# Spreading per-head values over partitions by DMA through DRAM instead of by matmul

## The chip, the core and the metric

The kernel runs on one core of one Trainium2 chip. The metric is the device time of one execution in microseconds (us), the median of three runs. A profile comes from one further execution, whose own time and span are given beside it. The core has five engines with a queue each: PE (TensorE, matmuls; its weight loads are listed as PEld), DVE (VectorE), ACT (ScalarE), POOL (GpSimd) and SP (SyncE), which here only issues DMAs.

## The reference, cut to what matters

The input `x` is 64 graphs of 256 tokens by 512 features, in float32, and `adj` is one 256x256 mask for each graph. Two graph-attention layers follow one another, each added to its input:

```python
h = relu(layernorm(x));  m = h @ map_w.T                 # layer 0, 8 heads of 64
n = m_head / max(norm(m_head), 1e-8)
cos_adj = ((n @ n.T) * keep > 0.1)
p = softmax(where(adj, -1e10, q @ k.T / 8)) * keep
x = x + relu(((cos_adj * p) @ sem) @ gcn_W.T / ((cos_adj * p).sum(-1) + 1))
h = relu(layernorm(x))                                   # layer 1, 4 heads of 64
x = x + (softmax(where(adj, q1 @ k1.T / 8, -max)) @ v1) @ Wo + bo
```

Two quantities belong to a head and a token and have to reach all 64 features of that head: the inverse length of a head in layer 0, by which `m` is multiplied to give `n`, and the inverse sum of the softmax in layer 1.

## The kernel before, in words

Everything is held with features (or keys) on the 128 partitions and the 256 tokens along the free axis, so the two heads of a chunk lie on partitions 0 to 63 and 64 to 127. Layer 0 has four chunks of two heads, layer 1 has two.

The graphs go through a software pipeline, written out by hand in `period(i)` (L535 to L662). One period works on four graphs: layer 1's attention of graph i-1 (`b`), layer 0's attention of graph i (`g`), the projections of graph i+1 (`nx`), and loading and normalising graph i+2 (`n2`). The scheduler is off (`tc.manual_schedule()`, L668): each engine runs its instructions in the order in which the program writes them, and waits at its head for whatever that instruction needs. In the trace a period in the middle of the run lasts from 1819.11 to 1877.92 us.

PSUM is one ring of eight banks (`ring`, L172; `bank`, L178). Tiles take the banks in turn, so a new tile waits until the tile eight allocations earlier has been read for the last time.

The order of PE in a period, with the lines that matter here:

- `sc1`: layer 1's scores of `b` (`products`, L384). ACT takes their exponentials (L391), and DVE masks them (L398).
- `p_b`: `spread(g)` (L357). Four matmuls against a selection matrix `sel` carry the inverse lengths `rn` of graph i to all partitions, into two banks; DVE multiplies `mT` by them into `nT` (L367).
- `p_m`, then `sc`: the first product of `mapped(nx)`, then layer 0's scores of `g`. ACT takes exponentials, DVE masks them (L400), POOL adds the two halves of each (`d`, L404).
- the rest of `mapped(nx)`. `seven_products` computes a 2x2 block product with seven matmul groups. Three of them add up in one bank, named `_z`; DVE reads that bank out between them (L291, L309), and the next group may only start when it has.
- `co`: the cosines `nT` x `nT` (L421). They take eight banks. DVE compares and multiplies (L434).
- queries of `nx`, the squares and `p_n` (their sums per head, `norms`, L350: four matmuls with 32 output columns each).
- `av` of layer 1 (`values1`) and `zb` (`sums1`, L514): layer 1's sums of `b`. `zb` is four matmuls against ones of 64 columns, so that each sum stands on all 64 partitions of its head. ACT copies it to `b.z` (L522), and `divided(b)` (L524) takes a reciprocal of 128x512 on DVE (L526) and multiplies `avs1` (L527).
- `av` and `sm` of layer 0, then the first product of `keys(nx)`, `sums_back` and `heads_back` (`p_l`, L483). For `heads_back` DVE makes `o` (L485), and POOL adds it to `xs` (L487, two instructions).
- the other products of `keys(nx)` (`p_k_z`, `p_k`), with `result(b)` (`p_o`, L532) among them. Its input is `avs1`.
- layer 1's projections of `g`, and the transposes of `n2`.

SP's queue in a period holds, in this order: four transposing DMAs `far` (L437), two transposing DMAs `mask` for `n2` (L327, which wait for `adb` of POOL, L322), the output of `b` (L636), and the loads of graph i+3 (L188, L190). The load into `xs` waits until the output has landed, since it reuses that buffer.

Of the kernel before, what the change touches and what calls it, by code (L numbers as in the profile page):

```python
# [8 lines left out]
F32 = mybir.dt.float32  # L9
# [19 lines left out]
class Weights:  # L29
# [4 lines left out]
    def __init__(self, nc, const, a):  # L34
        P, D, DH = 128, a["x"].shape[2], 64
        self.nc, self.const, self.a = nc, const, a
        self.ident = const.tile([P, P], F32, name="ident")
        make_identity(nc, self.ident)

        self.gt = const.tile([P, P], F32, name="gt")  # L40
        nc.vector.memset(self.gt, 0.0)
        for j in range(2):
            nc.scalar.dma_start(out=self.gt[j * DH:(j + 1) * DH, j * DH:(j + 1) * DH], in_=a["gcn_WT"])
        self.gb = const.tile([P, D // P], F32, name="gb")
        nc.scalar.dma_start(out=self.gb, in_=a["gcn_map_b"].rearrange("(c p) -> p c", p=P))
# [10 lines left out]
        self.sel = const.tile([P, 2, P], F32, name="sel")  # L56
        for j in range(2):
            nc.vector.memset(self.blk32[j * DH:(j + 1) * DH, j * 16:(j + 1) * 16], 1.0)
            for k in range(2):
                r = 32 * k + 16 * j  # L60
                nc.vector.tensor_add(self.sel[:, k, j * DH:(j + 1) * DH], self.ident[:, r:r + 1].to_broadcast([P, DH]),
                                     self.ident[:, r + DH:r + DH + 1].to_broadcast([P, DH]))
# [90 lines left out]
def fast_path(ctx, tc, a, w, chk, out):  # L153
# [4 lines left out]
    nc = tc.nc  # L158
# [2 lines left out]
    P, DH = 128, 64  # L161
    H0, NKC = D // DH, D // P
    INNER = a["Wq"].shape[1]
    NIC = INNER // P
    NT = S // P
    SCALE = DH ** -0.5

# [1 line left out]
    sb2 = ctx.enter_context(tc.tile_pool(name="sb2", bufs=2))  # L169
    sb1 = ctx.enter_context(tc.tile_pool(name="sb1", bufs=1))  # L170
    small = ctx.enter_context(tc.tile_pool(name="small", bufs=4))
    ring = ctx.enter_context(tc.tile_pool(name="ring", bufs=8, space=bass.MemoryType.PSUM))  # L172

    x_t = x.rearrange("b (t p) d -> b p t d", p=P)
# [3 lines left out]
    def bank(name, shape=(P, 2, S), dtype=F32):  # L178
        return ring.tile(list(shape), dtype, tag="bank", name=name)
# [173 lines left out]
    def lengths(g, p):  # L353
        g.rn = sb1.tile([P, S], F32, tag="rn", name=f"rn{g.i}")
        nc.vector.tensor_scalar_max(g.rn, p, COS_EPS * COS_EPS)

    def spread(g):  # L357

        ps = [bank(f"p_b{g.i}_{h}") for h in range(2)]
        for k in range(2):  # L360
            for h in range(2):
                r = slice(h * DH, (h + 1) * DH)
                nc.tensor.matmul(ps[h][:, k, :], w.sel[r, k, :], g.rn[r, :], start=True, stop=True)
        g.nT = sb1.tile([P, NKC, S], F32, tag="nT", name=f"nT{g.i}")
        for h in range(2):
            c = slice(2 * h, 2 * h + 2)
            nc.vector.tensor_mul(g.nT[:, c, :], g.mT[:, c, :], ps[h])  # L367

    def queries(g):
        g.qT = sb1.tile([P, NKC, S], F32, tag="qT", name=f"qT{g.i}")  # L370
# [108 lines left out]
    def heads_back(g):  # L479
        for t in range(NT):  # L480
            p = bank(f"p_l{g.i}_{t}", [P, NKC, P])
            for c in range(NKC):
                nc.tensor.transpose(p[:, c, :], g.avs[:, c, t * P:(t + 1) * P], w.ident)  # L483
            o = sb2.tile([P, H0, DH], F32, tag="xn", name=f"o{g.i}_{t}")
            nc.vector.tensor_mul(o, p.rearrange("p c (h d) -> p (c h) d", d=DH),  # L485
                                 g.rk[:, t, :, None].to_broadcast([P, H0, DH]))
            nc.gpsimd.tensor_add(g.xs[:, t, :], g.xs[:, t, :], o.rearrange("p h d -> p (h d)"))  # L487
# [8 lines left out]
    def values_in(g, t):  # L496
        if t == 0:
            g.v = sb1.tile([P, NT, INNER], F32, tag="v", name=f"v{g.i}")
            g.p_v = bank(f"p_v{g.i}", [P, NT, INNER])
        for c in range(NKC):  # L500
            nc.tensor.matmul(g.p_v[:, t, :], g.h1T[:, c, t * P:(t + 1) * P], w.wv1[:, c, :],  # L501
                             start=(c == 0), stop=(c == NKC - 1))
        if t == NT - 1:
            nc.vector.tensor_copy(g.v, g.p_v)
# [7 lines left out]
        nc.scalar.copy(b.avs1, av)  # L512

    def sums1(b):  # L514
        zb = bank(f"zb{b.i}")
        for c in range(NIC):
            last = NT - 1 if b.last else 0
            for m in range(last + 1):
                for s in range(2):
                    part = b.e1[c][:, s, m * S:(m + 1) * S] if b.last else b.d1[c][:, s, :]  # L520
                    nc.tensor.matmul(zb[s * DH:(s + 1) * DH, c, :], w.ones, part, start=(m == 0), stop=(m == last))
# [13 lines left out]
    def period(i):  # L535
# [8 lines left out]
        if b:  # L544
# [123 lines left out]
    with tc.manual_schedule():  # L668
# [36 lines left out]
            next(step)  # L705
        nc.scalar.activation(g.rn, g.rn, AF.Sqrt)
        nc.vector.reciprocal(g.rn, g.rn)
        if B > 1:
            edges(graphs[1])
            normal(1)  # L710
        nc.scalar.activation(spare[:, 1:], spare[:, :1], AF.Exp)
        for _ in range(4):
            next(s)
        if B > 1:
            normal_input(graphs[1])
        for i in range(B + 1):
# [299 lines left out]
```

## Time and profile before

| | |
|---|---|
| time, median of 3 runs | 3835.53 us (3833.66 to 3836.0) |
| the profiled execution: its own time, and its span | 3832.88 us, 3831.2 us |
| PE busy | 3786.6 us (99% of the span) |
| DVE, ACT, POOL busy | 2961.6, 1614.9, 2331.2 us |
| granted TensorE clock, mean | 0.997 |
| `p_b` (L363): PE busy, and DVE's multiplication (L367) | 66.0 us, 81.4 us in 128 |
| `zb` (L521) in 63 periods | 65.8 us |
| reciprocal 128x512 (L526) in 63 periods | 210.8 us, 3346 ns each |

The page gives for each group of instructions the busy time, the mean of one, and how long the engine stood idle before them. A busy PE only says that matmuls were in flight. The chain that ended last is followed back from the end, at each step to what released it; its shares say which engine set the pace. "Issue to landing" of a DMA is the time from its instruction on SP to the last increment of its semaphore. In the timeline the columns are start, length, engine, line, operation, output<-input, shape and count; in brackets stands the idle time before it and what ended it. Instructions that follow one another on an engine overlap there by some 0.08 us.

### The profile page before, as it was taken

How to read it: one execution, taken by the hardware profiler on the slowest of the kernel's cores; microseconds unless marked ns; L12 is line 12 of the kernel's file. 1: busy time of each engine (PE TensorE's matmuls, PEld its weight loads, DVE VectorE, ACT ScalarE, POOL GpSimd, SP SyncE). 2: the span in 40 equal slices, each digit the busy share in tenths (PEclk: the TensorE clock that was granted, in tenths of full speed). 3: DMA queues.
4: the chain of work that ended last, by engine and by line, in shares of the span. 5: the costliest groups of instructions: out<-in, count | busy, mean ns of one | idle time of the engine just before them, and what ended most of it. 6: DMA issues, size and time to landing. Idle time of an engine off the chain costs nothing.

```text
span 3831.2 us, 76121 instructions
## 1 busy us (share of the span) xinstructions
PE 3786.6 (99%) x30161; PEld 3215.8 (84%) x30161; DVE 2961.6 (77%) x5420; ACT 1614.9 (42%) x4108; POOL 2331.2 (61%) x2044
## 2 busy tenths in 40 slices
PE   8999999999999999999999999999999999999997
PEld 7888888888888888888888888888888888888885
DVE  6777777787777777877877778778777787787775
ACT  2444444444344444444444444444444444444443
POOL 3656566566565665665666656656666566566562
PEclk9999999999999999999999999999999999999999
DMA  3010000001101000011011000110010101101100
GB/s 96 24 31 20 30 27 26 30 21 31 31 21 29 27 26 30 21 31 30 21 28 31 22 30 21 31 30 21 29 33 20 30 21 31 30 21 30 32 14 21
DMA packets 171305, 108.05 MB, mean 28 GB/s; under 512 B 132673, under 2 KB 137281, under 8 KB 170945
## 3 DMA queue, kind: packets, MB, share of 16 engines
q1 hardware_dynamic: 168672, 103.09, 9.3%
q8 instruction: 241, 3.95, 0.4%
q14 instruction: 120, 0.97, 0.1%
q10 hardware_dynamic: 2272, 0.04, 0.0%
HBM read 44.34 MB, written 33.55 MB: 20 GB/s over the span
## 4 chain that ended last, share of the span: by engine, by line
PE 97%; DVE 1%; DMA 1%; issue 0%; POOL 0%; ACT 0%; SPq 0%; DVEq 0%; ACTq 0%
PE sc L384 9%; PE av L411 9%; PE p_q L266 6%; PE p_k L266 6%; PE p_m L266 6%; PE p_qk L266 6%; PE p_v L501 6%; PE p_o L532 6%; PE p_s L261 6%; PE p_m_z L266 5%; PE co L421 5%; PE p_s_z L261 5%; PE p_qk_z L266 4%; PE p_k_z L266 4%; PE p_q_z L266 4%; PE p_t L220 3%
## 5 line engine op out<-in xcount | busy, mean ns | idle before, releaser
L404 POOL TENSOR_TENSOR d<-e 128x512 f32<-128x512 f32 x382 | 659.5, 1753 | 85.3 <-DVE e L400 77.3
L244 POOL TENSOR_TENSOR sh<-hT 128x256 f32<-128x256 f32 x128 | 93.1, 728 | 766.3 <-ACT hT L221 766.3
L400 DVE TENSOR_TENSOR e<-e,mask 128x1024 f32<-128x1024 f32 x256 | 443.2, 1751 | 40.2 <-ACT e L391 40.2
L446 POOL TENSOR_TENSOR d<-d,e 128x512 f32<-128x512 f32 x252 | 320.9, 1273 | 222.0 <-DVE e L444 222.0
L391 ACT ACTIVATE e<-sc 128x512 f32<-128x512 f32 x768 | 389.8, 619 | 31.2 <-PE sc L384 31.2
L487 POOL TENSOR_TENSOR xs<-xs,o 128x512 f32<-128x512 f32 x128 | 159.8, 1271 | 362.3 <-DVE o L485 362.3
L439 POOL TENSOR_TENSOR d<-d,e 128x512 f32<-128x512 f32 x252 | 311.7, 1268 | 0.0
L398 DVE SCALAR_TENSOR_TENSOR e<-mask,e 128x1024 f32<-128x1024 bf16 x128 | 189.3, 1517 | 150.1 <-ACT e L391 150.1
L221 ACT ACTIVATE hT<-p_t 128x512 f32<-128x512 f32 x256 | 139.0, 595 | 390.1 <-PE p_t L220 390.1
L434 DVE SCALAR_TENSOR_TENSOR e<-co,e 128x256 f32<-128x256 f32 (+1 forms) x1024 | 276.6, 346 | 0.3 <-ACT up L431 0.3
L431 ACT ACTIVATE up<-co,below 128x128 bf16<-128x128 f32 x512 | 159.7, 363 | 241.1 <-PE co L421 235.3
L501 PE MATMUL p_v<-wv,hT 128*128 128x256 f32 x1024 | 242.2, 379 | 0.0
L384 PE MATMUL sc<-qT,kT 64*128 64x256 f32 x2048 | 239.0, 383 | 0.0
L532 PE MATMUL p_o<-wo,own 128*128 128x512 f32 x512 | 232.1, 596 | 3.1 <-DVE own L527 3.1
L411 PE MATMUL av<-e,sem 128*64 128x256 f32 x2048 | 232.1, 379 | 0.0
L444 DVE SCALAR_TENSOR_TENSOR e<-far,e 128x256 f32<-128x256 bf16 x256 | 229.5, 897 | 0.0
L512 ACT COPY own<-av 128x512 f32<-128x512 f32 x64 | 37.4, 585 | 455.3 <-PE av L411 442.0
L211 DVE TENSOR_SCALAR xn<-xs,mv,rs 128x512 f32<-128x512 f32 x256 | 229.0, 935 | 0.1
L526 DVE RECIPROCAL own<-own 128x512 f32<-128x512 f32 (+1 forms) x65 | 214.3, 3297 | 5.8 <-ACT own L522 5.8
L384 PEld LDWEIGHTS sc<-qT,kT 64*128 64x128 f32 x2048 | 193.1, 187 | 28.1 <-DVE nT L367 0.6
L198 DVE BATCH_NORM_STATS2 st<-xs 128x6 f32<-128x512 f32 x256 | 174.4, 681 | 52.5 <-POOL xs L487 49.4
L411 PEld LDWEIGHTS av<-e,sem 128*64 128x64 f32 x2048 | 147.2, 137 | 74.3 <-issue 0.6
(197 smaller groups left out, 9336.8 us busy)
## 6 DMA issues: line engine op xcount, KB each, us to landing
xs<-in_x_dram SPq DMA_DIRECT2D x64, 512.0 KB, 3.7
out_dram<-xs SPq DMA_DIRECT2D x63, 512.0 KB, 2.7
ad<-in_adj_dram SPq DMA_DIRECT2D x64, 64.0 KB, 3.5
far<-up SPq DMA_TRANSPOSE x256, 2.3
mask<-adb SPq DMA_TRANSPOSE x128, 2.3
wm<-in_L_gnn_map_w_dram SPq DMA_DIRECT2D x4, 256.0 KB, 3.3
gw<-in_L_gnn_gcn_map_w_dram SPq DMA_DIRECT2D x2, 512.0 KB, 5.5
wq<-in_L_gnn_q_w_dram SPq DMA_DIRECT2D x4, 256.0 KB, 6.4
```

What stands on the lines that cost most here:

```text
L261: nc.tensor.matmul(region, src[:, c, :], wt[:, block, c, :], start=p not in opened, stop=True, skip_group_check=True)
L266: nc.tensor.matmul(region[:, f, :], wt[:, block, c, f * P:(f + 1) * P], src[:, c, :], start=p not in opened, stop=True, skip_group_check=True)
L384: nc.tensor.matmul(ps[s][:, j, :], rows[h, c, j * P:(j + 1) * P], cols[h, c, :], start=True, stop=True)
L391: nc.scalar.activation(e[:, s, :], p.rearrange("p j q -> p (j q)"), AF.Exp, scale=SCALE)
L400: nc.vector.tensor_mul(e, e, m)
L404: nc.gpsimd.tensor_add(d, e[:, :, :S], e[:, :, S:])
L411: nc.tensor.matmul(av[s * DH:(s + 1) * DH, n, :], vs[:, j, (h0 + s) * DH:(h0 + s + 1) * DH], q[:, s, j * S:(j + 1) * S], start=(j == 0), s ...
L434: nc.vector.scalar_tensor_tensor(e, p.rearrange("p j q -> p (j q)")[:, lo:hi], THRESHOLD, e, op0=ALU.is_gt, op1=ALU.mult)
L439: nc.gpsimd.tensor_add(g.d[c], g.d[c], g.e[c][:, :, :S])
L446: nc.gpsimd.tensor_add(g.d[c], g.d[c], g.e[c][:, :, S:])
L501: nc.tensor.matmul(g.p_v[:, t, :], g.h1T[:, c, t * P:(t + 1) * P], w.wv1[:, c, :], start=(c == 0), stop=(c == NKC - 1))
L532: nc.tensor.matmul(p, b.avs1[:, c, t * P:(t + 1) * P], w.wo1[:, c, :], start=(c == 0), stop=(c == NIC - 1))
```

## The change

Both matmul spreads go. A new helper `by_head` writes one row for each head to DRAM and reads it back with the row repeated over 64 partitions, in two DMAs, one for each half of the partitions. All three DMAs stand on SP, and the two reads need the write to have landed.

- `spread` is now three DMAs: 8 rows of `rn` to DRAM, and two reads of 256 KB into `nT`. It is called at the end of period i-1, after the reciprocal of `nx.rn`, and so stands on SP after the loads of graph i+2. The multiplication is a new `units`: one DVE instruction of 128x1024, in place on `nT`, after the last `values_in` of the period.
- `sums1` has the form of `norms`: four matmuls of 32 columns into a bank of 128x256. ACT copies that to `rz`, DVE takes a reciprocal of 128x256, and `by_head` brings 4 rows to `b.z` with two reads of 128 KB. These DMAs stand on SP after the two `mask` transposes.
- `divided` is only the multiplication, and stands after `heads_back(g)`, ahead of the second product of `keys(nx)`.
- The check value of `b` is taken from `rz`. The constants `sel` go. Two fewer PSUM banks are taken in a period.

```diff
+    def by_head(rows, step, dst, name):
+        n = P // step
+        by = dram.tile([n // 2, 2, S], F32, tag=f"by{step}", name=f"by_{name}")
+        nc.sync.dma_start(out=by.rearrange("c s q -> (c s) q"), in_=rows[::step, :])
+        for s in range(2):
+            nc.sync.dma_start(out=dst[s * DH:(s + 1) * DH], in_=by[None, :, s, :].to_broadcast([DH, n // 2, S]))
+
     def spread(g):
-        ps = [bank(f"p_b{g.i}_{h}") for h in range(2)]
-        for k in range(2):
-            for h in range(2):
-                r = slice(h * DH, (h + 1) * DH)
-                nc.tensor.matmul(ps[h][:, k, :], w.sel[r, k, :], g.rn[r, :], start=True, stop=True)
         g.nT = sb1.tile([P, NKC, S], F32, tag="nT", name=f"nT{g.i}")
-        for h in range(2):
-            c = slice(2 * h, 2 * h + 2)
-            nc.vector.tensor_mul(g.nT[:, c, :], g.mT[:, c, :], ps[h])
+        by_head(g.rn, 16, g.nT, f"rn{g.i}")
+
+    def units(g):
+        nc.vector.tensor_mul(g.nT, g.nT, g.mT)
...
     def sums1(b):
-        zb = bank(f"zb{b.i}")
-        for c in range(NIC):
-            last = NT - 1 if b.last else 0
-            for m in range(last + 1):
-                for s in range(2):
-                    part = b.e1[c][:, s, m * S:(m + 1) * S] if b.last else b.d1[c][:, s, :]
-                    nc.tensor.matmul(zb[s * DH:(s + 1) * DH, c, :], w.ones, part, start=(m == 0), stop=(m == last))
-        nc.scalar.activation(b.z, zb, AF.Copy, accum_out=chk[:, b.i, 2:3])
+        zb = bank(f"zb{b.i}", [P, S])
+        last = NT - 1 if b.last else 0
+        for m in range(last + 1):
+            for h in range(H1):
+                c, s = divmod(h, 2)
+                part = b.e1[c][:, s, m * S:(m + 1) * S] if b.last else b.d1[c][:, s, :]
+                nc.tensor.matmul(zb[32 * h:32 * (h + 1), :], w.ones[:, :32], part, start=(m == 0), stop=(m == last))
+        b.rz = sb1.tile([P, S], F32, tag="rz", name=f"rz{b.i}")
+        nc.scalar.activation(b.rz, zb, AF.Copy, accum_out=chk[:, b.i, 2:3])
+        nc.vector.reciprocal(b.rz, b.rz)
+        by_head(b.rz, 32, b.z, f"rz{b.i}")

     def divided(b):
-        for q in (slice(0, P), slice(P, S)) if b.last else (slice(0, S),):
-            nc.vector.reciprocal(b.z[:, :, q], b.z[:, :, q])
-            nc.vector.tensor_mul(b.avs1[:, :, q], b.avs1[:, :, q], b.z[:, :, q])
+        nc.vector.tensor_mul(b.avs1, b.avs1, b.z)
...
-        if g:
-            spread(g)
         if nx:
             m, s = mapped(nx), messages(nx)
...
             sums1(b)
-            divided(b)
...
         if b:
-            nc.scalar.activation(b.z, b.z, AF.Copy, accum_out=chk[:, b.i, 3:4])
+            nc.scalar.activation(b.rz, b.rz, AF.Copy, accum_out=chk[:, b.i, 3:4])
         if g:
             sums_back(g)
             heads_back(g)
+        if b:
+            divided(b)
         if nx:
             next(k)
...
             nc.vector.reciprocal(nx.rn, nx.rn)
+            spread(nx)
...
+        if nx:
+            units(nx)
         if n2:
             normal_input(n2)
```

More of the change, by code (lines that the diff above doesn't have):

```diff
@@ L55, in __init__ @@
         nc.vector.memset(self.blk32, 0.0)
-        self.sel = const.tile([P, 2, P], F32, name="sel")
         for j in range(2):
             nc.vector.memset(self.blk32[j * DH:(j + 1) * DH, j * 16:(j + 1) * 16], 1.0)
-            for k in range(2):
-                r = 32 * k + 16 * j
-                nc.vector.tensor_add(self.sel[:, k, j * DH:(j + 1) * DH], self.ident[:, r:r + 1].to_broadcast([P, DH]),
-                                     self.ident[:, r + DH:r + DH + 1].to_broadcast([P, DH]))
         self.two = const.tile([P, 2, 32], F32, name="two")
@@ L163, in fast_path @@
     INNER = a["Wq"].shape[1]
-    NIC = INNER // P
+    H1, NIC = INNER // DH, INNER // P
     NT = S // P
@@ L171, in fast_path @@
     small = ctx.enter_context(tc.tile_pool(name="small", bufs=4))
+    dram = ctx.enter_context(tc.tile_pool(name="dram", bufs=2, space=bass.MemoryType.DRAM))
     ring = ctx.enter_context(tc.tile_pool(name="ring", bufs=8, space=bass.MemoryType.PSUM))
@@ L355, in lengths @@
         nc.vector.tensor_scalar_max(g.rn, p, COS_EPS * COS_EPS)
-    def spread(g):
-        ps = [bank(f"p_b{g.i}_{h}") for h in range(2)]
-        for k in range(2):
-            for h in range(2):
-                r = slice(h * DH, (h + 1) * DH)
-                nc.tensor.matmul(ps[h][:, k, :], w.sel[r, k, :], g.rn[r, :], start=True, stop=True)
+    def by_head(rows, step, dst, name):
[4 more added lines that the diff above has]
+            nc.sync.dma_start(out=dst[s * DH:(s + 1) * DH], in_=by[None, :, s, :].to_broadcast([DH, n // 2, S]))
+    def spread(g):
         g.nT = sb1.tile([P, NKC, S], F32, tag="nT", name=f"nT{g.i}")
-        for h in range(2):
-            c = slice(2 * h, 2 * h + 2)
-            nc.vector.tensor_mul(g.nT[:, c, :], g.mT[:, c, :], ps[h])
+        by_head(g.rn, 16, g.nT, f"rn{g.i}")
+    def units(g):
+        nc.vector.tensor_mul(g.nT, g.nT, g.mT)
     def queries(g):
@@ L707, in fast_path @@
         nc.vector.reciprocal(g.rn, g.rn)
+        spread(g)
         if B > 1:
@@ L713, in fast_path @@
             next(s)
+        units(g)
         if B > 1:
```

## The prediction

> **What bounds the kernel now.** I read the page's chain first, then the waits, then the chain and the timelines of one period (1819.11 to 1877.92 us, 58.81 us long; 62 of the 64 graphs' periods look like it), and last SP's queue and the DMAs. The page's chain:
>
> ```profile
> PE 97%; DVE 1%; DMA 1%; issue 0%; POOL 0%; ACT 0%; SPq 0%; DVEq 0%; ACTq 0%
> ```
>
> PE sets the pace and stands still nowhere in a middle period, so work taken from it counts only where its partners can follow sooner. The chain of that period (start, length, piece) gives the prices:
>
> ```profile
> 1821.11 0.86 PE p_b L363 x8
> ...
> 1847.80 0.57 PE p_n L350 x8
> 1848.37 1.88 PE av L411 x16
> 1850.24 0.86 PE zb L521 x8
> 1851.11 3.45 PE av L411 x32
> 1854.56 1.00 PE sm L462 x16
> ```
>
> `p_b` takes 0.86 us of the chain (its busy time, 66.0 us over 64 graphs, counts overlaps), `zb` 0.86, and `p_n`, which has the form the new `zb` gets, 0.57. Beside `p_b`, DVE and POOL (first lines DVE, L404 POOL):
>
> ```profile
> 1826.16 3.47 DVE L400 TENSOR_TENSOR e<-e,mask 128x1024 f32<-128x1024 f32 x2 [0.60 <-ACT e L391]
> 1832.56 1.50 DVE L400 TENSOR_TENSOR e<-e,mask 128x1024 f32<-128x1024 f32 x1
> 1834.98 0.41 DVE L291 TENSOR_TENSOR mT<-p_m_z,u4p_m 128x256 f32<-128x256 f32 x1
> 1828.58 7.84 POOL L404 TENSOR_TENSOR d<-e 128x512 f32<-128x512 f32 x4 [1.16 <-DVE e L400]
> ```
>
> POOL's additions of this shape take 1.27 us elsewhere (L439); here four take 7.84, 1.96 each. Two engines block each other. Plainer, three DVE masks and three POOL additions later on:
>
> ```profile
> 1846.99 0.98 DVE L444 SCALAR_TENSOR_TENSOR e<-far,e 128x256 f32<-128x256 bf16 x1
> 1850.26 1.40 DVE L444 SCALAR_TENSOR_TENSOR e<-far,e 128x256 f32<-128x256 bf16 x1
> 1846.42 1.27 POOL L446 TENSOR_TENSOR d<-d,e 128x512 f32<-128x512 f32 x1 [2.23 <-DVE e L444]
> 1850.10 1.27 POOL L446 TENSOR_TENSOR d<-d,e 128x512 f32<-128x512 f32 x1 [0.71 <-DVE e L444]
> ```
>
> The masks end at 1847.97 and 1851.66, each 0.28 us after POOL's addition (1847.69, 1851.37), though one alone takes 0.41. POOL runs undisturbed; DVE waits. Last, where the new `divided` will stand, and SP just before it:
>
> ```profile
> 1859.20 2.50 POOL L487 TENSOR_TENSOR xs<-xs,o 128x512 f32<-128x512 f32 x2 [5.29 <-DVE o L485]
> 1859.64 0.42 DVE L291 TENSOR_TENSOR kT<-p_k_z,u2p_k 128x256 f32<-128x256 f32 x1
> 1861.15 1.06 PE L266 MATMUL p_k_z<-sm,wk 128*128 128x128 f32 x8
> 1853.69 2.46 SPq L327 DMA_TRANSPOSE mask<-adb  x2
> ```
>
> [...] 16 passes of `av` after `p_n` take 1.88 against 1.73 elsewhere (3.45 for 32). [...] SP issues the load of `xs` at 1869.15, after the output issued at 1866.40 landed (2.7 us). [...]
>
> **The change part by part**, for a middle period.
>
> *`p_b` goes*: 0.86 us less on PE. After it `p_m`, `sc` and ACT's exponentials come 0.86 earlier. DVE and POOL don't. Their chain starts at DVE's L398 (1821.39), which waits for `sc1`, ahead of `p_b`. From 1821.6 [...] L398 and L400 at 1.08 each, L246 and L247 at 0.70, L404 at 1.27. From POOL's L245 (ends 1821.62) to the end of the last L400: 1.08+0.70+1.08+0.70+4x(1.27+1.09) = 13.0, so 1834.6 by this sum, 1834.06 in the trace. The 1.27 of DVE's L367, which goes, lay in a gap before its exponentials came. With them earlier, [...] a second addition comes between: the second L400 ends at 1829.56 against 1829.63. Little is won. PE waits for this chain twice: `p_m_z`'s second group needs `mT` out (1829.97; PE would be there 0.86 before 1830.32, at 1829.46), and the sixth bank of `co` is that of `p_m_z`, eight allocations back, read last at 1835.39; PE reaches it now at 1835.5, some 0.1 later. So of 0.86 about 0.16 is kept (0.1 slack, 0.06 earlier); bounds 0 and 0.86.
>
> *`zb` in 32-column form*: 0.57 against 0.86, [...]0.10 before, as `av` ahead of `sm`; 0.05 after[...]: 0.14 less; bounds 0 and 0.29.
>
> *DVE*: reciprocal 128x256 at 1.74 (as L649) instead of 3.35, 1.6 less in a stretch where DVE next waits for `rt` of PE anyway: nothing. ACT's copy shrinks from 0.60 to 0.38: nothing, and its check copy (1858.60) comes after the row's write.
>
> *The way to `b.z`*: the reciprocal runs 1853.71 to 1855.45, but SP is in the transposes until 1856.15. Then the write, its landing, and two reads of 128 KB. Output of 256 KB lands in 2.0, of 512 KB in 2.7, so 256 KB cost 0.7 and a write of 4 KB 1.3 to 2.0. Loads of 512 KB land in 3.7 (best 3.4), less 1.4 for their data: 2.0 to 2.3. The second read is issued 0.37 later: low end 2.0+0.35, high end 2.3+0.7. Landing: 1856.2+1.3+2.35 = 1859.85 to 1856.2+2.0+3.0 = 1861.2, middle 1860.5. No row shows a write read back at once; hence both ends.
>
> *`divided` moves* behind `o` [...]; POOL's two L487 stand there back to back, 0.14 earlier than now: 1859.06 to 1860.33, and on to 1861.57. If `b.z` lands before 1860.33, [...] ends at 1860.90, `kT` out at 1861.24, and PE starts `p_k_z` at 1861.30 instead of 1861.01 (1861.15 less the 0.14): 0.29 lost. If it lands later, DVE waits for the second: 1862.14, 1862.48, PE at 1862.54: 1.53 lost. Behind `divided` on DVE stand `kT` out, the moments and `xn`; `p_t` needs `xn` at 1866.9 then, and DVE has it by 1866.3, so nothing is added. `p_o`, whose input `divided` makes, comes 0.89 later still: covered.
>
> *`spread` and `units`*: SP is free for the row at 1870 to 1870.9 (after the output, `xs` and `ad`, 1.33), the reciprocal ends at 1869.86; the write queues behind the loads (landed 1873.3), 2x256 KB of reads need some 3.5 more: 1877. `units` (1.21, as one undisturbed L400) stands after L504 (ends 1877.85) in DVE's gap of 2.36 before L398, and ends by 1879.2. Hidden; a landing over 1 us later would push L398 and all that follows one for one. `far` comes on SP only at 1894.
>
> *Ends*: the first `p_b` 0.9 less. In the drain the masks are 1.15 sooner (DVE bound: L367 and its PE work gone), `xn` 0.55 later [...]. In the last period nothing hides the way: write and reads cost 3.8, `zb` and the split reciprocal save about 1.4: 2.4 more. Together +0.9.
>
> **Sum.** I take the late landing, since 0.87 of the 1.35 us between my ends lies after 1860.33; landings scatter (output 2.7 to 3.3), so one period in six gets through: (5x1.53+0.29)/6 = 1.32. Then 1.32-0.16-0.14 = +1.02 in 62 periods, +63, with the ends +64. The profiled execution took 3832.88, so 3897; the median is 2.65 above it: 3900. All periods late gives 3913, half of them 3876.
>
> **Rivals.** *Early landing* (27%): `b.z` lands before POOL's first L487 ends in nearly all periods; 0.29-0.30, about nothing, up to +0.2 with stragglers: 3836 to 3848. For it: output shows 1.3 as fixed cost; against it: the margin is 0.5 at the best end. *PE keeps its matmuls* (11%), the other side: [...] all 0.86 of `p_b` comes home, with early landing: 0.29-1.00 = -0.71, -44 and the ends: 3792. It decides itself at a loss of 1.0 at `p_k_z`; against it stands the price of L404, 1.96. *Later still* (12%): the row's write starts only when the transposes have landed (2.3 after issue, 1857.26), or repeated reads of one row are slow; past 1861.57 every 0.1 us costs 6: 3922 to 3980. *The late landing itself* has 50%: 3862 to 3922.
>
> **How the numbers follow.** 3830 to 3925 leaves out the fast case and two thirds of the last, 19%. A measurement of this kernel can tell about 0.2%, 7.7 us. Faster is the second rival, 11%; within 0.2% the lower half of early landing, 12%; slower the rest, 77%.
>
> **What would show it.** Right: `p_b` gone, but PE waiting before `p_m_z` (for DVE's `mT`) and in `co`; `divided` lasting over 1.2 us and ending 0.6 after POOL's second L487; PE waiting for `kT`; a period near 59.8. Wrong: no wait at `co` [...], `divided` ending near 1860.9 (early), DVE waiting for `nT`'s DMA at L398, or a write landing in 2.5 and more.

## The result, and the profile after

The changed kernel takes 3926.77 us, the median of four runs (3919.65 to 3933.4); the kernel before 3835.15 beside it. The ratio is 1.0239, with a 95% interval from 1.0221 to 1.0257: 91.6 us slower. The forecast was 3900 in a range from 3830 to 3925. The direction was right; the size was too small by 27 us, and the time lies 1.8 us outside the range. The profiled execution took 3926.56 us, its span 3924.7.

The page's chain of the changed kernel, against 97% PE before:

```profile
PE 73%; POOL 9%; DMA 6%; DVE 5%; issue 3%; ACT 3%; SPq 0%; DVEq 0%; ACTq 0%; POOLq 0%
```

PE no longer sets the pace alone: a fifth of the chain runs over POOL, DVE and a DMA. The waits name the places (engine, line, what it waited for; us in total, times, the longest):

```profile
DVE own L529 <- DMA own<-by_rz: 123.1, 63, 3.1
PEld p_k_z L261 <- DVE kT L286: 104.2, 62, 2.7
PE p_k_z L261 <- DVE kT L286: 92.3, 61, 2.5
DVE nT L367 <- DMA nT<-by_rn: 22.9, 35, 2.0
PEld p_m_z L261 <- DVE mT L286: 22.6, 38, 1.4
```

None of these stood in the profile of before. The weight load ahead of `p_k_z` shows the stall whole: 104.2 / 62 = 1.68 us a period. The chain of one period goes through it (start, length, piece):

```profile
1847.52 2.98 DMA own<-by_rz
...
1850.60 0.06 DVE own L529
...
1851.21 0.42 DVE kT L286
...
1851.68 1.16 PE p_k_z L261 x8
```

The timeline of the same place in the same period, the stretch that was shown of before around `heads_back`:

```profile
1842.61 2.46 SPq L322 DMA_TRANSPOSE mask<-adb  x2
1845.16 0.56 SPq L356 DMA_DIRECT2D by_rz<-rz  x1
1846.87 1.43 SPq L358 DMA_DIRECT2D own<-by_rz  x2
1848.25 2.49 POOL L487 TENSOR_TENSOR xs<-xs,o 128x512 f32<-128x512 f32 x2 [5.42 <-DVE o L485]
1850.60 0.69 DVE L529 TENSOR_TENSOR own<-own 128x512 f32<-128x512 f32 x1 [1.84 <-DMA own<-by_rz]
1851.21 0.41 DVE L286 TENSOR_TENSOR kT<-p_k_z,u2p_k 128x256 f32<-128x256 f32 x1
1851.68 1.16 PE L261 MATMUL p_k_z<-sm,wk 128*128 128x128 f32 x8 [1.32 <-DVE kT L286]
```

(`own` is the tile that holds `b.avs1` and `b.z`.) The row's write goes out at 1845.16, behind the transposes. The reads follow at 1846.87, once the write has landed (over the trace SP waits 70.0 us for it at 64 reads). DVE gets `b.z` only at 1850.60, when POOL's two additions are all but over (1850.74), and ends at 1851.29. Then `kT`, then PE. After its wait, PE's eight matmuls last 1.16 us, not 1.06.

So it is in most periods. `divided` (min/median/max, ns) over the whole trace:

```profile
L529 DVE TENSOR_TENSOR own<-own x64: 691/693/1374, 155.5 to 3910.6; 128x512 f32<-128x512 f32 x64
```

With POOL's additions left out it takes 0.68 to 0.69 us in a run below. Here it takes 0.69 in the median and 0.75 in the mean, so its turn against POOL costs the changed kernel only some 0.06 us a period (an estimate, from these two means). What PE waits for is the row's landing.

`zb` and what follows it, from the timeline:

```profile
1839.36 0.64 PE L522 MATMUL zb<-d,ones 128*32 128x256 f32 x8
1839.93 3.67 PE L411 MATMUL av<-e,sem 128*64 128x256 f32 x32
1843.54 1.07 PE L462 MATMUL sm<-d,two 128*32 128x256 f32 x16
```

From start to start, in the median, `zb` now takes 0.57 us against 0.86 before, the `av` ahead of it 1.88 against 1.78, and the `av` after it 3.60 against 3.55: 0.14 less.

And the masks and additions after `p_b` has gone:

```profile
1874.36 11.34 POOL L404 TENSOR_TENSOR d<-e 128x512 f32<-128x512 f32 x6
1874.75 4.17 DVE L400 TENSOR_TENSOR e<-e,mask 128x1024 f32<-128x1024 f32 x2 [0.93 <-ACT e L391]
1878.84 0.41 DVE L286 TENSOR_TENSOR mT<-p_m_z,u2p_m 128x256 f32<-128x256 f32 x1
1879.31 1.16 PE L261 MATMUL p_m_z<-sh,wm 128*128 128x128 f32 x8 [0.25 <-DVE mT L286]
```

POOL's six additions run without a gap, 1.89 each. `mT` stands on DVE behind the second L400, and PE waits for it at `p_m_z`.

Here is a period cut at PE's own marks, mean over 59 periods of each trace, in us (`p_k_z` and `p_m_z` are their second groups; the rows are kernels run below):

| kernel | `p_n` to `p_k_z` | to `p_o` | to `p_t` | to `sc1` | to `p_m_z` | to `p_q` | to next `p_n` | period |
|---|---|---|---|---|---|---|---|---|
| before | 13.42 | 0.89 | 3.44 | 12.44 | 11.21 | 6.42 | 10.99 | 58.82 |
| after | 14.96 | 1.02 | 3.55 | 12.44 | 10.70 | 6.49 | 11.13 | 60.31 |
| spread only | 13.42 | 0.89 | 3.44 | 12.44 | 10.70 | 6.50 | 11.13 | 58.52 |
| rows first | 14.77 | 1.00 | 3.44 | 12.44 | 10.71 | 6.50 | 11.13 | 59.99 |
| no transfer | 13.42 | 0.89 | 3.44 | 12.44 | 10.76 | 6.53 | 10.99 | 58.47 |
| no transfer, short masks | 13.42 | 0.89 | 3.44 | 12.44 | 10.34 | 6.43 | 11.00 | 57.96 |
| rows early, `divided` later | 13.28 | 0.92 | 3.44 | 12.44 | 10.76 | 6.53 | 11.00 | 58.37 |
| the same, sums later | 13.28 | 0.92 | 3.44 | 12.44 | 10.34 | 6.42 | 11.00 | 57.85 |
| spread only, sums later | 13.42 | 0.89 | 3.44 | 12.44 | 10.34 | 6.42 | 10.99 | 57.95 |

After minus before: +1.54 at `p_k_z`, +0.13 in its restart and the way to `p_o`, +0.11 before `p_t`, -0.30 in the three columns that `p_b` touches: +1.48 a period, 92 us in 62.

The +0.11 before `p_t` is no wait of `p_t`. It comes from five periods in which the matmuls of `p_o` (in two of them those of `p_k_z` too) run slower. One of them, and a stretch of it with what the engines did (the last three figures are the granted clock, the DMAs' share and GB/s):

```profile
403.08 5.29 PE L534 MATMUL p_o<-wo,own 128*128 128x512 f32 x8
```

```profile
403.60:406.90 3.30, 3.30 (x6) 1.24 (x5) 2.70 (x9) 2.09 (x5) 0.00 (x0) 0.50 0.00 0
```

`p_o` lasts 3.60 us elsewhere; here the granted clock is 0.50. The five periods cost some 1.7 us each, 8 in all, 0.14 a period in the mean. Each had waited over 2.0 us at `p_k_z`; four other periods had too, and kept their clock.

### The profile page after: what moved, and what is told of

The parts are those of the page before. It is cut to its first block, busy times and chain, and to the rows that moved or that the text cites. A ratio compares the mean times of both kernels' runs of the same rounds, so it can differ in the third digit from the quotient of the medians.

```text
span 3924.7 us, 75985 instructions
## 1 busy us (share of the span) xinstructions
PE 3766.1 (96%) x29649; PEld 3148.4 (80%) x29649; DVE 2891.7 (74%) x5350; ACT 1589.2 (40%) x4108; POOL 2417.0 (62%) x2044
## 3 DMA queue, kind: packets, MB, share of 16 engines
q14 instruction: 125, 1.02, 0.1%
## 4 chain that ended last, share of the span: by engine, by line
PE 73%; POOL 9%; DMA 6%; DVE 5%; issue 3%; ACT 3%; SPq 0%; DVEq 0%; ACTq 0%; POOLq 0%
PE av L411 9%; PE p_o L534 6%; PE p_qk L261 6%; PE p_v L501 6%; POOL d L404 5%; DMA own<-by_rz 5%; PE p_q L261 5%; PE p_s L256 5%; PE p_s_z L256 5%; PE p_qk_z L261 4%; PE p_q_z L261 4%; PE p_k_z L261 3%; PE p_k L261 3%; PE co L421 3%; DVE e L400 3%
## 5 line engine op out<-in xcount | busy, mean ns | idle before, releaser
L404 POOL TENSOR_TENSOR d<-e 128x512 f32<-128x512 f32 x382 | 725.3, 1932 | 12.0 <-DVE e L398 8.0
L239 POOL TENSOR_TENSOR sh<-hT 128x256 f32<-128x256 f32 x128 | 109.2, 853 | 887.2 <-ACT hT L216 887.2
L400 DVE TENSOR_TENSOR e<-e,mask 128x1024 f32<-128x1024 f32 x256 | 478.5, 1889 | 52.3 <-ACT e L391 52.1
L534 PE MATMUL p_o<-wo,own 128*128 128x512 f32 x512 | 241.1, 615 | 11.3 <-DVE own L529 11.3
L398 DVE SCALAR_TENSOR_TENSOR e<-mask,e 128x1024 f32<-128x1024 bf16 x128 | 196.9, 1577 | 52.5 <-ACT e L391 52.5
L261 PE MATMUL p_k_z<-sm,wk 128*128 128x128 f32 x1024 | 144.0, 284 | 92.4 <-DVE kT L286 92.3
L384 PEld LDWEIGHTS sc<-qT,kT 64*128 64x128 f32 x2048 | 192.9, 187 | 27.5
L261 PEld LDWEIGHTS p_k_z<-sm,wk 128*128 128x128 f32 x1024 | 126.2, 194 | 104.2 <-DVE kT L286 104.2
```

The lines of the kernel that those rows point to most:

```text
L261: nc.tensor.matmul(region[:, f, :], wt[:, block, c, f * P:(f + 1) * P], src[:, c, :], start=p not in opened, stop=True, skip_group_check=True)
L384: nc.tensor.matmul(ps[s][:, j, :], rows[h, c, j * P:(j + 1) * P], cols[h, c, :], start=True, stop=True)
L400: nc.vector.tensor_mul(e, e, m)
L404: nc.gpsimd.tensor_add(d, e[:, :, :S], e[:, :, S:])
L534: nc.tensor.matmul(p, b.avs1[:, c, t * P:(t + 1) * P], w.wo1[:, c, :], start=(c == 0), stop=(c == NIC - 1))
```

## The experiments

The theory: the loss sits at `p_k_z`, where `divided` waits for its DMA and, if the row lands while POOL adds, for its turn against POOL (0.69 us for `divided` without an addition beside it, 1.40 behind one, both below); of `p_b` the turns of DVE's masks and POOL's additions keep most. The runs show these turns and their lengths, and none shows what the two engines take turns at. The rivals were that the DMAs themselves cost the time (SP's queue, `nT` late, traffic), and that PE waits for something else. Edits are against the changed kernel unless it says otherwise.

### Each half alone

Only `spread` by DMA; `zb` and `divided` as before, so that nothing of `by_rz` is left.

```diff
     def sums1(b):
-        ... (32 columns, rz, by_head(b.rz, 32, b.z, ...))
+        ... (as before: ones of 64 columns, b.z straight from zb)
     def divided(b):
-        nc.vector.tensor_mul(b.avs1, b.avs1, b.z)
+        ... (as before: reciprocal and multiplication, behind sums1)
```

> Only the lengths go by DMA (spread and units as in the change); layer 1's sums and their division stay as before. Theory [...]: what p_b gave up, 0.86 us a period, is mostly lost again to the turn-taking of DVE's masks and POOL's additions, so 0.16 us a period or 10 us in all is won, and late landings of nT (DVE waited for them 22.9 us in the changed kernel) give some back: 3822 to 3842 us. Rival (PE keeps what is taken from it): 0.86 in 62 periods is 53 us: 3775 to 3800 us. Rival (this part carries much of the loss): above 3860 us.

Measured 3810.62 us (3807.45 to 3811.42), ratio 0.9935 [0.9918, 0.9951]. It lies between the two expectations: `p_b` gives 0.30 us a period, where I had 0.16 and the rival 0.86. The waits of this kernel:

```profile
PEld p_m_z L261 <- DVE mT L286: 23.0, 42, 0.8
DVE nT L367 <- DMA nT<-by_rn: 19.0, 32, 1.7
```

There is a wait at `p_m_z`, as forecast. None of a bank in `co` is listed, and that one was forecast too. So the first half is a gain of 24 us, and all of the loss, 116 us above this run, comes with the second half.

`divided` behind the second product of `keys(nx)`, so that `kT` is out first:

```diff
             heads_back(g)
-        if b:
-            divided(b)
         if nx:
             next(k)
+        if b:
+            divided(b)
```

> The changed kernel with the multiplication by b.z one step later, behind the second product of the keys, so that the read-out of that product doesn't stand behind it on DVE. Theory: the wait of PE for kT (about 1.5 us in 61 periods of the changed kernel) goes; p_o, which needs the multiplication, waits some 0.25 us instead: 3927 - 62 x 1.25 = about 3850 us (3835 to 3865). Rival (the loss lies elsewhere and the wait at kT only covers it): above 3890 us.

Measured 3856.49 us (3853.07 to 3857.73), ratio 1.0054 [1.0037, 1.0071], as the theory had it: 70 us of the loss are gone with `divided` out of `kT`'s way. `p_k_z` has no wait, and the one at `p_o` is:

```profile
PE p_o L534 <- DVE own L529: 36.4, 62, 8.5
```

Without the longest that is 27.9 / 61 = 0.46 us a period. `b.z` is late for `p_o` as well; behind `kT` its lateness costs less.

### The turn against POOL, and the stragglers

The row's write ahead of the two `mask` transposes on SP (`turned_mask` holds the transposes that `edges` issued):

```diff
             sums1(b)
+        if n2:
+            turned_mask(n2)
```

> The changed kernel with the two mask transposes of a period issued behind the rows of the sums on SP, so that the row's write starts some 0.75 us sooner (reciprocal at its end instead of the transposes). b.z should land about 0.75 us sooner. Theory 1 ([...] DVE's multiplication waits for the second of POOL's additions into xs anyway): at most 0.1 us a period, 3918 to 3930 us. Theory 2 (the landing sets it): 0.75 in 62 periods is 46 us: 3875 to 3890 us.

Measured 3910.53 us (3906.66 to 3914.84), ratio 1.0195 [1.0178, 1.0212]: below the range of the first theory, and far above that of the second. The write goes out 0.76 us sooner and `b.z` lands 0.77 sooner, 12.97 us after `p_n` and not 13.74 (medians). Yet `p_k_z` starts at 14.76 in the median, against 14.82. POOL's first addition ends at 12.60 in both and its second at 13.83, so this landing meets the second, and now `divided` waits for it: 1.398 us in the median, not 0.693. What the earlier row gave, the turn against POOL took. What went is the tail: `p_k_z` starts at 15.46 in the slowest tenth of periods of the changed kernel, and at 14.77 here. So 16 us of the loss came with landings past the end of the second addition; no middle period of this run has the half clock, which was some 8 us in the changed kernel's profile.

The same with POOL's additions of `o` taken out:

```diff
                                  g.rk[:, t, :, None].to_broadcast([P, H0, DH]))
-            nc.gpsimd.tensor_add(g.xs[:, t, :], g.xs[:, t, :], o.rearrange("p h d -> p (h d)"))
```

> As the run with the rows first, and POOL's two additions of o into xs left out (layer 0's result is not added to x), so that no addition of POOL stands beside the multiplication. Theory 1 [...]: against the run with the additions the multiplication comes at once on landing, some 0.75 us sooner: 35 to 50 us less than that run, about 3875 us. Theory 2 (landing alone): no difference to that run, within 8 us.

Measured 3879.97 us (3876.21 to 3881.91), ratio 1.0115 [1.0098, 1.0132]: 31 us less, near the 35 to 50 expected if the turn sets the stall, where the landing alone was to give none. The durations of `divided` (min/median/max, ns) in the two kernels, the one with the additions first:

```profile
L532 DVE TENSOR_TENSOR own<-own x64: 691/1398/1766, 157.7 to 3897.6; 128x512 f32<-128x512 f32 x64
```

```profile
L531 DVE TENSOR_TENSOR own<-own x64: 681/693/694, 157.6 to 3865.4; 128x512 f32<-128x512 f32 x64
```

POOL's additions are what makes this instruction 0.7 us longer: without them it never lasts above 0.694. The timeline of the kernel with them shows one such turn:

```profile
1836.68 2.49 POOL L490 TENSOR_TENSOR xs<-xs,o 128x512 f32<-128x512 f32 x2 [5.43 <-DVE o L488]
1838.45 1.27 DVE L532 TENSOR_TENSOR own<-own 128x512 f32<-128x512 f32 x1 [1.26 <-DMA own<-by_rz]
```

POOL ends at 1839.17, DVE at 1839.72, 0.55 later, though it has had its data since 1838.45.

But most of the stall stays without the additions. PE's wait at `p_k_z` in the two kernels, again the one with them first:

```profile
PEld p_k_z L261 <- DVE kT L286: 94.3, 62, 1.9
```

```profile
PEld p_k_z L261 <- DVE kT L286: 61.7, 61, 2.1
```

That is 1.52 us a period against 1.01: without a turn against POOL two thirds of the stall would still be there, from the late row alone.

### What keeps `p_b`

`spread` left out (ACT copies `mT` to `nT`), with `zb` and `divided` as before; then the same with masks of 256 columns in place of 1024:

```diff
     def units(g):
-        nc.vector.tensor_mul(g.nT, g.nT, g.mT)
+        nc.scalar.copy(g.nT, g.mT)
...                                     # the second kernel also:
-            nc.vector.tensor_mul(e, e, m)
+            nc.vector.tensor_mul(e[:, :, :P], e[:, :, :P], m[:, :, :P])
...                                     # and the mask of layer 1 (L398) alike
```

> The kernel before without any spread of the lengths: p_b and its multiplication are left out, and ACT copies mT to nT at the end of the period before (so the cosines are not normalised; leaves out that part of layer 0). Layer 1's sums as before. It frees PE of 0.86 us a period with no DMA in it. Theory [...]: DVE's masks and POOL's additions, [...] set when PE may go on, so only part comes home, like the 24 us of the run with the spread alone: 3800 to 3815 us. Rival (that run fell short because nT landed late): all 0.86 comes home, 53 us: 3775 to 3787 us.

> As the run without a spread, and DVE's six masks of a period (L398, L400) treat 256 of their 1024 columns (leaves out three quarters of the masking in both layers), [...]. Theory [...]: now all 0.86 us of p_b comes home: 3775 to 3787 us, some 25 us less than the run without a spread. Rival (PE's own order or ACT's exponentials set that stage): as the run without a spread, within 8 us.

Measured 3812.55 us (3812.23 to 3815.84), ratio 0.9949 [0.9933, 0.9966], and 3774.03 (3772.1 to 3774.93), ratio 0.9844 [0.9828, 0.9861]. The first is in the range of the theory; the second gains 39 us on it, where 25 were expected. Without any transfer for `nT` no more of `p_b` comes home than with it; so the transfer doesn't keep it. Its wait, in the first:

```profile
PEld p_m_z L260 <- DVE mT L285: 27.6, 62, 0.7
```

27.6 / 62 = 0.45 a period. With short masks this wait is gone and the period is 57.96, 0.86 below before: the whole of `p_b`. The table above places what was kept, 0.42 ahead of `p_m_z` and 0.10 behind, where its eight matmuls last 1.16 us after the wait and 1.06 without. It is DVE's time in this stretch that keeps `p_b`. Short masks don't yet tell a mask's own length from its turns with POOL; the last two runs do.

### The row early enough

`rz` reduced ahead of the moments of `n2` on DVE and written ahead of the transposes:

```diff
-            moments(n2, f"0_{n2.i}")
...
             sums1(b)
+        if n2:
+            turned_mask(n2)
+            moments(n2, f"0_{n2.i}")
```

> The changed kernel with the mask transposes behind the rows on SP, and the moments of graph i+2 behind the reciprocal of the sums on DVE, so that the reciprocal ends 1.75 us sooner and the row's write starts about 2.6 us sooner than in the changed kernel. The way to b.z takes 5.5 us there; b.z should land 0.5 us before DVE has made o, ahead of POOL's additions. Theory: no wait at kT is left (or the 0.3 us behind the first addition at most): 3927 - 14 (scatter) - 62 x 1.5 = about 3815 us (3805 to 3835). Rival (the stall is the place of the multiplication as such): above 3880 us.

And with the loads of graph i+3 behind `spread(nx)` on SP, so that `nT` has the queue to itself:

```diff
-        if i + 3 < B:
-            graphs[i + 3] = load(i + 3)
...
             spread(nx)
+        if i + 3 < B:
+            graphs[i + 3] = load(i + 3)
```

> As the run with the rows early, and the loads of graph i+3 behind the spread of the lengths on SP, so that the 8 KB row is not queued behind 576 KB of loads. Theory: DVE no longer waits for nT (19 to 23 us in all in the runs with it), and the scatter of the periods goes: 5 to 15 us less than the run with the rows early, about 3803 us. Rival (nT was hidden): the same within 5 us.

Measured 3845.67 us (3843.72 to 3849.62), ratio 1.0033 [1.002, 1.0047], and 3845.22 (3841.48 to 3849.9), ratio 1.0033 [1.0019, 1.0047]. The first missed what I had expected by 30 us: 81 us were won, but `p_k_z` still waits. DVE is at `divided` before its turn, finds POOL's first addition running, and ends 0.55 after it. This is the early landing of the prediction, priced there at 0.29 a period; 0.26 is measured (13.54 against 13.28 without it). On top, some periods fall back to the late case. The timeline of the second kernel holds both, the late one first:

```profile
1800.75 2.49 POOL L490 TENSOR_TENSOR xs<-xs,o 128x512 f32<-128x512 f32 x2 [5.45 <-DVE o L488]
...
1860.65 2.95 POOL L490 TENSOR_TENSOR xs<-xs,o 128x512 f32<-128x512 f32 x2 [5.42 <-DVE o L488]
```

```profile
1802.35 1.44 DVE L532 TENSOR_TENSOR own<-own 128x512 f32<-128x512 f32 x1 [1.09 <-DMA own<-by_rz]
...
1861.08 1.39 DVE L532 TENSOR_TENSOR own<-own 128x512 f32<-128x512 f32 x1
```

At 1861.08 DVE comes between the two additions, and POOL is the one held up (2.95, not 2.49). At 1802.35 it comes after the second has begun. Nearly all its periods take one of two values, 58.69, or 59.91 in 9 of 59, and the difference of 1.22 is one addition of POOL. Why the row lands late in about one period of seven I have not found. In the second kernel DVE no longer waits for `nT` (but once, 0.4 us), and the time is the same, as the rival had it: `nT`'s lateness cost nothing that these runs can tell.

### Home again

`divided` behind the second keys product in that kernel; then POOL's additions of layer 1's halves (L404 for `b`) behind the first product of `mapped(nx)`, out of the way of the masks:

```diff
             heads_back(g)
-        if b:
-            divided(b)
         if nx:
             next(k)
+        if b:
+            divided(b)
```

```diff
-            else:
-                b.d1 = [halves(b.e1[c], f"1_{b.i}_{c}") for c in range(NIC)]
...
+        if b and not b.last:
+            b.d1 = [halves(b.e1[c], f"1_{b.i}_{c}") for c in range(NIC)]
```

> As the rows early with the loads later, and `divided` behind the second keys product, so that `kT` is out before it. The theory that the loss at `p_k_z` is the turn [...]: nothing of it is left, a row that lands one addition later costs only the few tenths by which `p_o` waits, and what was gained elsewhere (`p_b` in part, `zb`) shows: the period falls from two levels of 58.69 and 59.91 to one near 58.3, the time to 3800 to 3815. The rival, that the DMAs themselves (their issue on SP, their traffic) or the late `p_o` cost the time: 3835 to 3850, as in the run before.

> The same, and POOL's two additions of layer 1's halves (L404 for `b`) moved behind the first product of `mapped(nx)`, [...]. [...] some 0.5 us a period come home without leaving anything out: 3770 to 3785. If it is some other wait behind `p_m` or `sc`, the time stays within 5 us of the run without this move; if the additions are then late for `zb`, it is above it.

Measured 3810.04 us (3808.04 to 3812.38), ratio 0.9939 [0.9923, 0.9956], and 3777.17 (3775.56 to 3779.12), ratio 0.9853 [0.9836, 0.9869]. Both as expected. 33 us come from moving two POOL additions, with nothing left out. The mask of 128x1024 falls from 1.927 to 1.502 us in the mean, and PE's wait at `p_m_z` for `mT`, 27.5 us in 62 periods, is gone: it is DVE's turns against POOL that kept `p_b`. The control is that move alone, in the kernel before:

> The kernel before with only that move of POOL's two additions. PE binds there and stands still nowhere, [...]: 3827 to 3842. If the move by itself were worth something (the rival), 3800 to 3815, and the run with it would prove nothing on `p_b`.

Measured 3834.3 us (3831.76 to 3837.12), ratio 1.0002 [0.9993, 1.0011]: nothing, since PE stood still nowhere. And the first half of the change with that move, and the loads behind `spread`:

> Only the first half of the change (`spread` by DMA, `zb` and `divided` as before), with the loads of graph i+3 behind the DMAs of `spread`, and POOL's two additions moved. [...] all of the 0.86 of `p_b` comes home, 62 periods of 57.95: 3774 to 3785. The rival, that the transfer of `nT` binds next (it lands some 3.6 us into the period with the loads ahead of it): 3800 to 3815, with DVE waiting for the DMA at `units`.

Measured 3776.09 us (3774.0 to 3778.12), ratio 0.985 [0.9834, 0.9866], the fastest of the complete kernels together with the one before (3777.17), from which it can't be told. Its page:

```profile
PE 98%; DVE 1%; POOL 0%; DMA 0%; issue 0%; ACT 0%; DVEq 0%; ACTq 0%
...
L404 POOL TENSOR_TENSOR d<-e 128x512 f32<-128x512 f32 x382 | 600.4, 1592 | 191.5 <-DVE e L400 191.5
...
L400 DVE TENSOR_TENSOR e<-e,mask 128x1024 f32<-128x1024 f32 x256 | 379.8, 1505 | 61.4 <-ACT e L391 61.4
```

PE is the bound again. A mask L400 takes 1.505 us in the mean, against 1.902 in the run with the spread only: four a period, 1.6 us less on DVE. So the second half of the change, placed as in the run before, adds no gain that can be told.

### The length of the read

What was still open was the read of `b.z`, longer than forecast. One read over 128 partitions in place of two over 64:

```diff
-        by = dram.tile([n // 2, 2, S], F32, tag=f"by{step}", name=f"by_{name}")
-        nc.sync.dma_start(out=by.rearrange("c s q -> (c s) q"), in_=rows[::step, :])
-        for s in range(2):
-            nc.sync.dma_start(out=dst[s * DH:(s + 1) * DH], in_=by[None, :, s, :].to_broadcast([DH, n // 2, S]))
+        by = dram.tile([2, n // 2, S], F32, tag=f"by{step}", name=f"by_{name}")
+        nc.sync.dma_start(out=by.rearrange("s c q -> c s q"), in_=rows[::step, :])
+        nc.sync.dma_start(out=dst.rearrange("p c q -> p (c q)"),
+                          in_=by.rearrange("s c q -> s (c q)")[:, None, :].to_broadcast([2, DH, n // 2 * S]))
```

> The changed kernel with one read over all 128 partitions in `by_head` instead of two over 64 each. If the second instruction on SP is what makes the way long, the landing comes 0.6 us sooner, 4.8 instead of 5.4 us after the row's write: still behind POOL's first addition in most periods, so the median period stays near 60, but the stragglers fall inside the second addition and the time goes to 3905 to 3918. If the bytes set the landing, 256 KB in one DMA land as late as twice 128 KB: 5.3 to 5.5, and 3920 to 3930.

Measured 4731.18 us (4725.85 to 4738.94), ratio 1.2338 [1.2317, 1.2358]. Both expectations were far off. The timeline:

```profile
1912.65 0.52 SPq L357 DMA_DIRECT2D own<-by_rz  x1
1920.20 0.69 DVE L529 TENSOR_TENSOR own<-own 128x512 f32<-128x512 f32 x1 [5.98 <-DMA own<-by_rz]
```

The 256 KB take 7.55 us here, 7.32 in the median of all periods; the 512 KB of `nT`, which `by_head` now reads in one DMA too, 12.66. 256 KB more cost 5.34, so some 2.0 us don't depend on the size (an estimate from these two, if the cost goes with the bytes). A stretch in the middle of this read, and then half a microsecond of the two reads in the changed kernel, both by what was busy (the last two figures are the DMAs' share and GB/s):

```profile
1915.00:1918.00 3.00, 0.82 (x8) 0.63 (x6) 0.00 (x0) 1.91 (x3) 1.20 (x1) 1.00 0.13 51
```

```profile
1849.00:1849.50 0.50, 0.50 (x7) 0.50 (x6) 0.00 (x0) 0.00 (x0) 0.50 (x2) 1.00 0.65 223
```

The single read moves 51 GB/s and the two reads 223; 0.13 of 16 engines is two, 0.65 is ten (estimates from these shares). Why the single read keeps fewer of them busy, no run shows. The granted clock fell too, to 0.919 from 0.993. By the marks of the table a period of this run lasts 73.1 us. Against the 57.85 of the complete kernel that waits least, some 11 us of the difference lie ahead of `p_k_z` and `p_m_z`, where PE waits, and some 4 from there to `p_t` and `p_q`, where matmuls run slower (753 ns for one of `p_o` in the mean of the trace, 615 in the changed kernel).

Reads of a quarter of the columns:

```diff
+        w = S if step == 16 else S // 4
         for s in range(2):
-            nc.sync.dma_start(out=dst[s * DH:(s + 1) * DH], in_=by[None, :, s, :].to_broadcast([DH, n // 2, S]))
+            nc.sync.dma_start(out=dst[s * DH:(s + 1) * DH, :, :w], in_=by[None, :, s, :w].to_broadcast([DH, n // 2, w]))
...
-        nc.vector.tensor_mul(b.avs1, b.avs1, b.z)
+        w = S // 4
+        nc.vector.tensor_mul(b.avs1[:, :, :w], b.avs1[:, :, :w], b.z[:, :, :w])
```

> The changed kernel with both reads of layer 1's inverse sums cut to the first 64 of the 256 columns, and `divided` multiplying only these (three quarters of layer 1's division are left out). If the bytes cost, the landing after the second read's issue falls from 3.04 to some 2.3 us; if it is a part that does not depend on the size, it stays within 0.15 of 3.04. The time itself says little, [...]: 3880 to 3925.

From the second read's issue to DVE's start 2.65 us in the median, against 3.04 with all columns: between the two expectations. Three quarters of the bytes cost 0.39, so all of them some 0.5, and 2.5 us of the read don't depend on its size (estimates, if the cost goes with the bytes). It took 3887.77 us, in one run.

The single read in the kernel with the rows first:

> The run with the rows first (3910.5), and one read instead of two. There `b.z` landed 0.37 us after POOL's first addition ended. The threshold: a landing 0.4 or more sooner catches the place between the two additions, the median period falls by one addition, 1.23 us, to near 58.7, and the time to 3840 to 3870, with some periods still on the late level. If the landing does not move, or a few tenths here cost only a few tenths: 3885 to 3912.

Measured 4655.39 us (4654.25 to 4664.01), ratio 1.2145 [1.2125, 1.2165]: the same single read (DVE waits for it 297.2 us in 64 periods), which says nothing on the threshold. The threshold stands on the two levels seen above instead, 58.69 and 59.91.

## Why the prediction was right or wrong

**The stall at `p_k_z`: the place right, what sets it wrong, its size in part by luck.** `kT` stands behind `divided` on DVE, and PE waits for `kT`: that is as forecast. But `divided` was to wait for its row and then for POOL, and so to last over 1.2 us. It lasts 0.69 in the median, as it does without POOL's additions. The row lands so late that POOL's turn is all but over, and the row all but alone sets the stall. That the price of the late landing, 1.53 a period, is near the 1.68 measured is luck: the median landing falls just ahead of the end of POOL's second addition. Where the row lands sooner, in the run with the rows first, nearly every period is the case that was priced (1.398 us for `divided`), and it costs 14.77 - 13.28 = 1.49. The early landing was priced at 0.29 and is 0.26.

**The way to `b.z`: the step that failed.** The prediction gave 3.65 to 5.0 us from the write's issue to the landing. It took 5.4 in the median, to DVE's start. The write was inside its bounds: 1.70 to the first read's issue, where 1.3 to 2.0 stood. The reads were not: 0.66 to the second issue (0.37 was taken, from the loads), and 3.04 from there (some 2.0 to 2.6 was taken, from loads of 512 KB less their data). From the run with a quarter of the bytes, 2.5 of it is a part without bytes, larger than the 2.0 to 2.3 of that step. So the reads took 3.70 from the first issue, where 2.35 to 3.0 stood: this is the term that was too small. Why a read of a repeated row has the larger part without bytes, no run shows.

**"One period in six gets through": wrong.** None does: 5.4 us put the median landing 1.1 us behind the end of POOL's first addition, and 0.1 ahead of the end of the second, so the scatter ran over the other edge, in 21 of 61 periods. "All periods late", 3913 in the prediction, is what the run with the rows first shows (3910.5). The landings past the second addition, with the half clock behind some of them, add 16 us to that. (Half of the periods late gives 3874 by the prediction's own terms, not 3876.) My rival "later still", at 12%, had this price, every 0.1 us past the second addition, and its lower end is where the result fell; I should have given it more.

**`p_b`: the mechanism right, one place wrong, the size wrong.** The turns of DVE and POOL keep most of it; 0.30 comes home in the changed kernel, not 0.16. The second threshold, the sixth bank of `co`, shows in no wait: `co` starts after the wait at `p_m_z`, and so comes later by as much. Its absence is thus no sign that these turns cost nothing, though the prediction has it under "Wrong". Where two thresholds follow one another, the second has to be counted from the first. Of the 0.52 that the turns keep, 0.42 is the wait ahead of `p_m_z`, and 0.10 is its restart behind it, 1.16 us for eight matmuls and not 1.06, as at `p_k_z`.

**`zb` in 32 columns: right, in each term.** 0.14 forecast, and 13.42 - 13.28 = 0.14 measured where nothing waits: 0.29 less for `zb`, 0.10 and 0.05 more for the two `av` beside it. Why these take longer, no run shows.

**`nT` hidden: right in cost, wrong in time.** It was to land at 1877, 29.2 us after `p_n`. In the changed kernel `units` starts at 32.0 in the median, and DVE waits for the row in 35 periods, 22.9 us in all. The write, behind the loads, took 2.94 us to its reads and not 1.76, as with the loads behind it; and from the second read's issue some 4.2 pass. The gap before L398 takes most of it up. In the table, the spread only against no transfer, it costs 0.14 ahead of the next `p_n` and gives back 0.09 before that; the run with the loads later is no faster.

**Left out:** PE's restart, and its clock. A `p_k_z` that has waited lasts 0.10 us longer, which is 6 us in all. In five periods, each behind a wait of over 2.0 us, the granted clock is 0.50 for some 3 us, which costs another 8 us in all.

In sum against the forecast, over 62 periods: 1.68 and not 1.32 at `p_k_z` (+22 us), 0.13 and 0.11 from its restart to `p_t` (+15), 0.30 and not 0.16 from `p_b` (-9): 28 us, of which 27 were missing in the time.

## What to carry to other kernels

A value that goes to DRAM and back costs a write, its landing, and a read, 5.4 us here for 4 KB; count each from its own issue, and compare the sum with the edges of what stands there, not with their middle: a landing just behind the start of POOL's second addition cost 1.22 us a period, all at once. And ask which of two waits ends last: an earlier row was worth little (16 us) as long as the turn against POOL stood behind it. Put the consumer behind what the bound engine waits for (70 us here), and get the source out ahead of unrelated transfers on the queue (81 us here, with its reciprocal ahead of the moments as well). Time taken from the bound engine came home here only where the engines that turn it into work had the same slack: taking out the matmuls of `p_b` gave 24 us by itself, and two POOL additions moved out of the way another 33.

## What the runs showed that I had not expected

- A dependent read was issued 1.70 us after its write; behind the loads it was 2.94, with the loads behind it 1.76.
- A read of one row into 64 partitions kept SP for 0.60 us, where the load of 512 KB in the same period kept it for 0.39, and landed 3.04 us after its issue (128 KB), 2.5 of them without bytes (an estimate, from the run with a quarter of them).
- One read over all 128 partitions took 7.32 us for what two reads do in 3.70; in stretches of them the DMAs moved 51 and 223 GB/s.
- Two additions moved on POOL: nothing in a kernel bound by PE (1.0002), 33 us once the matmuls were gone.
- `divided` in the changed kernel hardly waits for POOL (0.06 us a period); with the row 0.77 us sooner it does (0.6), and in the median PE starts `p_k_z` only 0.06 sooner.
- A matmul group that had waited lasted 1.16 us, not 1.06; and in five periods behind a long wait PE had half its clock.
